# A four-layer graph stack on one Trainium2 core: variances of the layernorms in four segments, node rows and dense adjacency blocks written during mixing, and a first part of the convolution ahead of its product

## The chip, the cores and the metric

The kernel runs on one core of one Trainium2 chip. The metric is the device time of one execution in microseconds (us); lower is better. Five engines work side by side, each through its own list of instructions in order: PE multiplies matrices, DVE and ACT do vector work and can read PE's results, POOL does vector work and issues gathers, and SP issues plain memory transfers. A thing that one engine makes and another reads is handed over by a semaphore.

## The reference

Eight graphs of 2048 nodes with 64 features each share one adjacency matrix. Four layers each add their result to x, after a layernorm without weights and a relu:

```python
def _layernorm(x, axis=-1, eps=1e-5):
    m = jnp.mean(x, axis=axis, keepdims=True)
    v = jnp.var(x, axis=axis, keepdims=True)
    return (x - m) / jnp.sqrt(v + eps)
...
    h = jnp.maximum(_layernorm(x, axis=-1), 0.0)
    x = x + _L0_gnn_ref(h, ...)
    h = jnp.maximum(_layernorm(x, axis=-1), 0.0)
    x = x + _L1_gnn_ref(h, adj, L1_gnn_embedding, L1_gnn_weight, L1_gnn_bias)
    h = jnp.maximum(_layernorm(x, axis=-1), 0.0)
    x = x + _L2_gnn_ref(h, adj, ...)
    h = jnp.maximum(_layernorm(x, axis=-1), 0.0)
    x = x + _L3_gnn_ref(h, adj, L3_gnn_weight, L3_gnn_a, L3_gnn_bias)
```

Layer 0 is a hypergraph attention g and an industry average (a product with the adjacency), mixed by a softmax over two tanh scores. Layer 1 is the one that most of the change concerns:

```python
        As = [jnp.eye(N, dtype=x.dtype)]
        if K > 1:
            As.append(A)
        for _ in range(2, K):
            As.append(2.0 * (A @ As[-1]) - As[-2])
        A_stack = jnp.stack(As, 0)
        x_g = jnp.einsum('knm,bmc->bnkc', A_stack, x)
        out = jnp.einsum('bnki,nkio->bno', x_g, w)
        return out + b
```

Here K is 3 and the weights w of a node are a mixture of 16 sets by the node's embedding. Layer 2 makes three rounds of messages over the adjacency, layer 3 is an attention over neighbours.

## The kernel before

**Layout.** Features stand on the partitions, two graphs at a time: a tile is 128 partitions (2 graphs x 64 features) by nodes, and q (0 to 3, `NP`) counts the four pairs. Nodes go in 4 chunks of 512 (`CW`) or 16 tiles of 128 (`P`). "Node rows" are the transposed form, one node on a partition with 512 columns. Six large buffers, `q0` to `q5`, and some more by stage are shared by name (`Slots`).

**The norm.** `norm_parts` (L275) is a generator, so that callers can put other work between its halves. First half, for each pair: PE subtracts the mean (a product with `center`), ACT squares, relu on DVE or ACT. Then four products with `to_rows` (L261) put the variances of pair q into two rows of a group of 32 partitions, 512 columns; ACT takes the root (L290), DVE the reciprocal (L291). Second half, for each pair: a product with `from_rows` (L266) spreads the two rows over 128 partitions, and the caller's `write` multiplies. There are 17 norms: 4 at the start, beside the check of the adjacency (`check_adj`), 4 in mixing, 4 in the convolution and 5 in the third layer (`Scores.chunk`, the last two with 256 columns).

**Mixing** (`mix`, L695). For each chunk and pair, PE makes the scores p1 (two tiles of two PSUM banks), ACT their tanh, PE the difference pd (one bank), ACT t2, DVE the mixture. Three more banks, `bank`, serve everything else: the transposes that `each` makes of gathered rows, and the norm of the chunk before, whose halves are stepped at pairs 0 and 1. Work given as `beside` is stepped once a pair: `Lists.fill` (L2507), which gathers 60 blocks of the adjacency by index, four at a time, and stores them as `cells` in bfloat16. The write of the norm (L706) puts its result into `xe` and `xo`. x of the last chunk goes to buffers `q4`, `q5`.

**Second layer** (`layer1_near`, L1642). It begins with `lists.load`: three dense blocks of rows of the adjacency and 13 blocks called `zero` are loaded and cast to bfloat16. Then `xe` and `xo` are transposed to node rows `ah` (in `q4`, `q5`), which are also stored to `sent[0]`. The first adjacency product follows tile by tile (`Feed`): for each target a dense part with the three hub tiles, and a listed part, for which POOL gathers rows of `sent[0]`, ACT and DVE split each into two parts (L2630, L2631), and PE multiplies. `turn` transposes the result back. `acc` has three PSUM banks there.

**Convolution** (`convolution_near`, L1697). It loads its weights, then makes the second product for the first chunk whole (`product(0)`), then for each chunk and pair 16 outputs `pk` (8 blocks of weights, 2 halves, six banks): a product with w01 opens the bank, one with w2 on the second product closes it, DVE adds the bias and multiplies by the embedding (L1852), and POOL sums (L1858, the last block on DVE). Pieces of the next chunk's product are stepped in between.

**Order.** The program's order is the one written, but the scheduler may put an instruction earlier in its engine's list when its inputs are ready; `behind` keeps the order of those given to it. A buffer that is used again makes its next writer wait for the last reader.

Of the kernel before, what the change touches and what calls it, by code (L numbers as in the profile page):

```python
# [19 lines left out]
P = 128  # L20
NB = 8
# [4 lines left out]
R = P // NP  # L26
CW = 512
# [19 lines left out]
F16 = mybir.dt.float16  # L47

# [86 lines left out]
class Kernel:  # L135
# [76 lines left out]
    def setup(self):  # L212
# [19 lines left out]
        self.to_rows = c.tile([P, R], F, name="to_rows")  # L232
        nc.vector.memset(self.to_rows, 0.0)
        self.from_rows = c.tile([P, 2, D], F, name="from_rows")
        for s in range(2):
            nc.vector.memset(self.to_rows[s * D : (s + 1) * D, s : s + 1], 1.0 / D)
        for q in range(NP):
            r = slice(R * q, R * (q + 1))
            nc.vector.tensor_copy(
                self.from_rows[r],  # L240
                self.ident[r, R * q : R * q + 2].unsqueeze(2).to_broadcast([R, 2, D]),
            )
# [18 lines left out]
    def to_pair_rows(self, out, stationary, src):  # L261

        for q in range(NP):
            self.mm(out[R * q : R * (q + 1)], stationary, src(q))

    def from_pair_rows(self, out, q, rows):  # L266

        r = slice(R * q, R * (q + 1))
        self.mm(out, self.from_rows[r].rearrange("r s f -> r (s f)"), rows[r])
# [5 lines left out]
    def norm_parts(self, ch, x, xr, sq, std, bank, write, relus=None):  # L275
# [12 lines left out]
        pv = bank()  # L288
        self.to_pair_rows(pv, self.to_rows, lambda q: sq[:, q])
# [3 lines left out]
        for q in range(NP):  # L293
            pr = bank()
            self.from_pair_rows(pr, q, std)
# [377 lines left out]
    def x_ind(self, slots, k):  # L673
        w_ind = self.block_diag(k, self.a["W_ind"], "w_ind")
        x_ind = Split(slots, "x_ind", ("q7", "q6", "q9", "q8"))
        hn = self.h[0]
        with self.tc.tile_pool(reuse_waits="tile", name="x_ps", bufs=3, space=PSUM) as ps:
# [17 lines left out]
    def mix(self, slots, ind, g, fcw, av, each=None, beside=None):  # L695
# [17 lines left out]
        with (  # L713
# [6 lines left out]
            def attend(ch, q):  # L720
# [9 lines left out]
                if q == 0:  # L730
                    bufs[ch] = end if ch == NC - 1 else [b[:, ch % 2] for b in big]
# [15 lines left out]
            for ch in range(NC):  # L747
                s = slice(ch * CW, (ch + 1) * CW)
                x, sq, xr = bufs[ch]
                for q in range(NP):  # L750
# [22 lines left out]
                    if q < 2:  # L773
                        next(norm, None)
                    next(beside, None)
                self.store_x(0, ch, x)
                std = w.tile([P, CW], F, name="std")
                norm = self.norm_parts(ch, x, xr, sq, std, bank, write, nc.scalar)
            for _ in norm:
                pass  # L780
            for _ in beside:
# [9 lines left out]
    def layer0_pairs(self, slots, far):  # L791
# [8 lines left out]
        with tc.tile_pool(reuse_waits="tile", name="k0", bufs=1) as k:  # L800
# [3 lines left out]
            with (  # L804
# [46 lines left out]
                x_ind = self.x_ind(slots, k1)  # L851
# [42 lines left out]
            )  # L894
            with tc.tile_pool(reuse_waits="tile", name="filling", bufs=1) as w:
                self.mix(slots, ind, h_t, fcw, av, each, lambda bank: self.lists.fill(cells, w))
# [119 lines left out]
    def layer0(self, slots):  # L1016
# [14 lines left out]
        with tc.tile_pool(reuse_waits="tile", name="k0", bufs=1) as k:  # L1031
            x_ind = self.x_ind(slots, k)
# [609 lines left out]
    def layer1_near(self, slots, k2, far):  # L1642
# [11 lines left out]
        with (  # L1654
            tc.tile_pool(reuse_waits="tile", name="cheb", bufs=2) as w,
# [1517 lines left out]
```

## Time and profile before

| what | value |
|---|---|
| median of 3 runs | 2005.93 us (2004.48 to 2013.83) |
| profiled execution | 2004.73 us, of which the span of the profile is 2003.0 |
| mean granted PE clock | 0.91 |
| busy, share of the span | PE 85%, DVE 70%, POOL 52%, ACT 40% |
| start and check of the adjacency | 0 to 101 us |
| hypergraph attention, lists, industry product | 101 to 458 |
| mixing | 458 to 593.5 |
| transposes to node rows, dense blocks | 593.5 to 611.3 |
| first product of the second layer | 611.3 to 721 |
| second product for the first chunk | 721 to 767 |
| convolution with the rest of the second product | 767 to 1245 |
| third layer | 1245 to 1710 |
| fourth layer | 1710 to 2003 |

Times in the table by stage are from the span's start, read from the first and last instruction of a line. A busy PE is not PE at its peak, since matmuls are pipelined; and idle time of an engine that isn't the bound costs nothing.

### The profile page before, as it was taken

What the parts mean: (1) busy time and instruction counts of PE and PEld (TensorE: products, weight loads), DVE (VectorE), ACT (ScalarE), POOL (GpSimd) and SP (SyncE); (2) the same over time, 40 slices, a digit from 0 to 9 for tenths busy, and PEclk for the clock granted to TensorE, in tenths of its full rate; (3) what the DMA queues carried; (4) which work ended last, traced back from release to release, by engine and by line L of the source; (5) the groups of instructions that cost most, each with busy time, mean ns of one, the idle gap of its engine ahead of it and who ended that gap; (6) DMA issues with size and microseconds to landing.
All of it is one profiled execution on the core that took longest, in us unless ns stands there. A gap on an engine that the chain in (4) does not pass through costs nothing. (4 is left out here: it accounts for less than half of the span.)

```text
span 2003.0 us, 22362 instructions
## 1 busy us (share of the span) xinstructions
PE 1712.0 (85%) x7094; PEld 986.7 (49%) x7098; DVE 1393.1 (70%) x2281; ACT 811.0 (40%) x1634; POOL 1036.1 (52%) x1005
## 2 busy tenths in 40 slices
PE   6888999898977779999999998678789899378985
PEld 2446766663325544444434443567576575244432
DVE  6888788864776657676776556698787566257874
ACT  5722545445555643221110101555556553176400
POOL 1101466668734645875765453553664440657870
PEclk8888999999887979999999899889899898689997
DMA  9641223336247864232320211667687674845665
GB/s 340 260 117 44 74 95 111 106 111 202 58 135 225 242 190 123 74 116 63 85 80 32 79 48 63 214 198 253 199 261 244 184 241 136 261 117 172 172 177 193
DMA packets 125882, 305.21 MB, mean 152 GB/s; under 512 B 29345, under 2 KB 33201, under 8 KB 120241
## 3 DMA queue, kind: packets, MB, share of 16 engines
q0 software_dynamic: 45328, 149.60, 25.0%
q1 hardware_dynamic: 78112, 149.80, 22.4%
q10 hardware_dynamic: 2304, 4.20, 0.6%
q8 instruction: 60, 0.98, 0.2%
q14 instruction: 78, 0.63, 0.1%
HBM read 240.40 MB, written 63.14 MB: 152 GB/s over the span
## 5 line engine op out<-in xcount | busy, mean ns | idle before, releaser
L2613 POOL DMA_INDIRECT raw<-sent,index x300 | 315.0, 1050 | 343.0 <-DVE part_lo L2631 137.7
L2631 DVE TENSOR_TENSOR part_lo<-raw,part_hi 128x512 fp32r<-128x512 f32 x352 | 266.2, 777 | 142.9 <-ACT part_hi L2630 77.4
L2630 ACT CAST part_hi<-raw 128x512 fp32r<-128x512 f32 x352 | 212.2, 619 | 333.1 <-PE acc L176 223.5
L1858 POOL TENSOR_TENSOR half<-half,y 128x512 f32<-128x512 f32 x192 | 247.6, 1319 | 135.0 <-DVE y L1852 134.3
L176 PE MATMUL pk<-q,w 128*128 128x512 f32 (+1 forms) x768 | 301.9, 610 | 2.3 <-DVE q L1742 0.9
L176 PE MATMUL acc<-q,ident 128*128 128x512 f32 x416 | 205.9, 620 | 25.3 <-issue 12.1
L176 PE MATMUL acc<-part_hi,weights 128*128 128x512 f32 x365 | 179.3, 495 | 31.8 <-ACT part_hi L2630 17.6
L176 PE MATMUL acc<-part_lo,weights 128*128 128x512 f32 x365 | 168.6, 464 | 36.2 <-DVE part_lo L2631 27.2
L1852 DVE SCALAR_TENSOR_TENSOR y<-pk,bias,q 128x512 f32<-128x512 f32 x224 | 157.8, 743 | 55.1 <-PE pk L176 36.1
L176 PEld LDWEIGHTS pk<-q,w 128*128 128x128 f32 (+1 forms) x768 | 115.9, 190 | 156.1 <-issue 121.0
L2862 POOL DMA_INDIRECT ring<-f_rows,near x121 | 138.9, 1148 | 71.0 <-issue 30.5
L176 PEld LDWEIGHTS acc<-q,ident 128*128 128x128 f32 x416 | 77.4, 196 | 102.0 <-issue 63.2
L176 PEld LDWEIGHTS acc<-part_lo,weights 128*128 128x128 f32 x365 | 75.1, 206 | 86.9 <-DVE part_lo L2631 50.5
L176 PEld LDWEIGHTS acc<-part_hi,weights 128*128 128x128 f32 x365 | 75.0, 206 | 82.4 <-issue 48.0
L2340 POOL TENSOR_TENSOR q<-q,beta 128x512 f32<-128x512 f32 x57 | 76.1, 1337 | 71.3 <-DVE beta L2316 32.9
L176 PE MATMUL pp<-adj,x_ind_hi 128*128 128x512 f32 x256 | 90.5, 470 | 0.5 <-DVE q L864 0.3
L2933 DVE TENSOR_TENSOR q<-ring,e 128x1024 f32<-128x1024 f32 x58 | 69.9, 1218 | 20.7 <-remote 10.0
L2599 ACT CAST hub_weights<-dense 128x384 fp32r<-128x384 bf16 x80 | 40.6, 511 | 104.1 <-PE acc L176 96.9
L2340 POOL TENSOR_TENSOR q<-q,coef 128x512 f32<-128x512 f32 x57 | 63.1, 1108 | 21.2 <-DVE q L2363 16.9
L291 DVE RECIPROCAL std<-std 128x512 f32<-128x512 f32 (+1 forms) x17 | 53.7, 3161 | 27.3 <-ACT std L290 23.4
L176 PE MATMUL pp<-adj,x_ind_lo 128*128 128x512 f32 x256 | 72.0, 400 | 0.0
L2524 POOL DMA_INDIRECT listed_raw<-in_adjT_dram,cell x60 | 62.2, 1037 | 16.5 <-issue 15.8
(501 smaller groups left out, 3430.8 us busy)
## 6 DMA issues: line engine op xcount, KB each, us to landing
rows<-in_adj_dram SPq DMA_DIRECT2D x16, 1024.0 KB
adj_t<-in_adjT_dram SPq DMA_DIRECT2D x64, 256.0 KB
own<-sent SPq DMA_DIRECT2D x52, 256.0 KB
raw<-sent SPq DMA_DIRECT2D x52, 256.0 KB
sent<-u SPq DMA_DIRECT2D x48, 256.0 KB
q<-x SPq DMA_DIRECT2D x9, 1024.0 KB
links<-squares POOLq DMA_DIRECT2D x16, 512.0 KB
x<-q SPq DMA_DIRECT2D x8, 1024.0 KB
```

The lines of the kernel that those rows point to most:

```text
L176: self.nc.tensor.matmul(out, lhsT, rhs, start=start, stop=stop)
L291: nc.vector.reciprocal(std, std)
L1852: nc.vector.scalar_tensor_tensor(y, pks[b, half], bias[:, b : b + 1], emb[:, b], op0=OP.add, op1=OP.mult,)
L1858: add.tensor_add(acc, acc, y)
L2340: self.nc.gpsimd.tensor_tensor(x, x, by.unsqueeze(2).to_broadcast([P, NB, D]), op=OP.mult)
L2524: self.kern.behind(nc.gpsimd.indirect_dma_start(raw[:, i], None, rows, bass.IndirectOffsetOnAxis(ap=self.cell[:, c + i : c + i + 1], axis= ...
L2599: self.nc.scalar.copy(to, self.lists.dense[:, :, i * P : (i + 1) * P])
L2613: self.nc.gpsimd.indirect_dma_start(raw, None, self.rows[:], bass.IndirectOffsetOnAxis(ap=self.lists.index[:, c : c + 1], axis=0),)
L2630: nc.scalar.copy(hi, raw)
L2631: nc.vector.tensor_sub(lo, raw, hi.bitcast(F))
L2862: self.nc.gpsimd.indirect_dma_start(to, None, self.kern.f_rows[:], bass.IndirectOffsetOnAxis(ap=index, axis=0))
L2933: nc.vector.tensor_tensor(y.rearrange("n i (b f) -> n i b f", b=NB), block[:, i : i + 2, : NB * D].rearrange("n i (b f) -> n i b f", b=NB) ...
```

## The change

- The variances of a norm go into four segments. A segment is a quarter of the columns. `to_rows` is wider (32+6 columns), and segment i is multiplied with a shifted part of it, so that its rows land two partitions further on; four products accumulate into one bank of 128 columns. Root and reciprocal run on 128 columns. The spreading takes a segment's two rows with `from_rows[:, i]` and writes a quarter of the bank.
- `mix` takes `turned`: at pairs 2 and 3 of a chunk the four node tiles of the chunk before are transposed from `xe`, `xo` into `ah` and stored to `sent[0]`, two a pair; the last four after the last norm. x of the last chunk uses the ring of buffers like the others.
- `fill` also loads the dense and zero blocks, in 16 pieces of 512 columns, and ACT copies them; cells, dense and zero are held as bytes. `load` is gone.
- The new class `Conv` holds weights and the embedding's buffer and is made ahead of the first product; embeddings are loaded at the ninth tile. For pair 0 of the first chunk `first_part` makes the products with w01 alone, adds the bias, multiplies and sums on DVE: 8 of 16 pieces after the first product, the rest between the pieces of `product(0)`. Later the products with w2 open their own banks, and are multiplied and added.
- PSUM: the two products and the convolution share one pool; `acc` and `side` have two banks together.
- The industry weights have their own pool (`x_ind`); the third layer's attention reuses the tile `mine` for its first output.

```diff
-        self.to_rows = c.tile([P, R], F, name="to_rows")
+        self.to_rows = c.tile([P, R + 2 * SEG - 2], F, name="to_rows")
         nc.vector.memset(self.to_rows, 0.0)
-        self.from_rows = c.tile([P, 2, D], F, name="from_rows")
+        self.from_rows = c.tile([P, SEG, 2, D], F, name="from_rows")
         for s in range(2):
-            nc.vector.memset(self.to_rows[s * D : (s + 1) * D, s : s + 1], 1.0 / D)
+            at = 2 * SEG - 2 + s
...
+            nc.vector.memset(self.to_rows[s * D : (s + 1) * D, at : at + 1], 1.0 / D)
         for q in range(NP):
             r = slice(R * q, R * (q + 1))
             nc.vector.tensor_copy(
-                self.from_rows[r],
-                self.ident[r, R * q : R * q + 2].unsqueeze(2).to_broadcast([R, 2, D]),
+                self.from_rows[r].rearrange("r i s f -> r (i s) f"),
+                self.ident[r, R * q : R * q + 2 * SEG].unsqueeze(2).to_broadcast([R, 2 * SEG, D]),
...
-        pv = bank()
-        self.to_pair_rows(pv, self.to_rows, lambda q: sq[:, q])
+        n = sq[:, 0].shape[-1] // SEG
+        std = std[:, :n]
+        parts = [slice(i * n, (i + 1) * n) for i in range(SEG)]
+        pv = bank()[:, :n]
+        for i, c in enumerate(parts):
+            at = 2 * (SEG - 1 - i)
+            self.to_pair_rows(
+                pv, self.to_rows[:, at : at + R], lambda q: sq[:, q][:, c], start=i == 0,
+                stop=i == SEG - 1,
+            )
         nc.scalar.activation(std, pv, AF.Sqrt, bias=self.eps)
         nc.vector.reciprocal(std, std)
         yield
         for q in range(NP):
             pr = bank()
-            self.from_pair_rows(pr, q, std)
+            for i, c in enumerate(parts):
+                self.from_pair_rows(pr[:, c], q, std, i)
             write(q, ch, xr[:, q], pr)
...
+                    last = ch == NC - 1 and turned is None
+                    bufs[ch] = end if last else [b[:, ch % 2] for b in big]
...
+                    elif ch > 0 and turned is not None:
+                        for i in range(2):
+                            turned((ch - 1) * TC + 2 * (q - 2) + i, bank)
...
+            if turned is not None:
+                for t in range(NT - TC, NT):
+                    turned(t, bank)
...
+            def turned(t, bank):
+                s = slice(t * P, (t + 1) * P)
+                for i, (src, h) in enumerate(((xo, slice(D, P)), (xe, slice(0, D)))):
+                    pt = bank()[:, : NP * D].rearrange("n (q f) -> n q f", q=NP)
+                    for q in range(NP):
+                        nc.tensor.transpose(pt[:, q], src(q)[h, s], self.ident[h, h])
+                    self.copy(columns(ah(t), i), pt)
+                nc.sync.dma_start(self.sent[0][s], ah(t))
...
-            lists.load(w)
-            hub = Hub(w, "first_hub")
-            for t in range(NT):
-                s = slice(t * P, (t + 1) * P)
-                for i, (src, h) in enumerate(((xo, hi), (xe, lo))):
-                    pt = ps.tile([P, NP, D], F, name="pt", tag=("acc", "pz")[i], bufs=3)
+            conv = Conv(self, slots, k, ps)
+            with tc.tile_pool(reuse_waits="tile", name="cheb", bufs=2) as w:
+                hub = Hub(w, "first_hub")
+                for t in range(HUBS):
+                    hub.fill(self, t, ah(t))
+
+                def turn(t):
+                    s = slice(t * P, (t + 1) * P)
+                    pz = ps.tile([P, NP, P], F, name="pz", tag="pk", bufs=6)
                     for q in range(NP):
-                        nc.tensor.transpose(pt[:, q], src(q)[h, s], ident[h, h])
-                    self.copy(columns(ah(t), i), pt)
-                nc.sync.dma_start(self.sent[0][s], ah(t))
-                if t < HUBS:
-                    hub.fill(self, t, ah(t))
...
+                    if t == NT // 2:
+                        conv.begin()
+                turn(NT - 1)
+                for _ in range(8):
+                    next(conv.early)
...
             for _ in product(0):
+                next(conv.early, None)
+            for _ in conv.early:
                 pass
...
+                                if not begun:
+                                    self.mm(pk, w01[half][:, c], src(q)[:, s], stop=False)
...
-                                self.mm(pks[b, half], w2[h, c], aah[h, q], start=False)
+                                self.mm(pks[b, half], w2[h, c], aah[h, q], start=begun)
...
+                                new = begun or b > 0
+                                y = w.tile([P, CW], F, name="y", bufs=3) if new else acc
+                                if begun:
+                                    nc.vector.tensor_mul(y, pks[b, half], emb[:, b])
+                                else:
+                                    nc.vector.scalar_tensor_tensor(
+                                        y, pks[b, half], bias[:, b : b + 1], emb[:, b],
+                                        op0=OP.add, op1=OP.mult,
+                                    )
+                                if new:
+                                    own = b == NBLK - 1
+                                    add = nc.vector if own else nc.gpsimd
                                     add.tensor_add(acc, acc, y)
                         if q == NP - 1 and not ends:
...
+        def take():
+            if blocks:
+                to, src = blocks.pop(0)
+                raw = w.tile([P, CW], F, name="block_raw", bufs=3)
+                if len(src.shape) == 3:
+                    raw = raw.rearrange("p (i n) -> p i n", n=P)[:, : src.shape[1]]
+                nc.sync.dma_start(raw, src)
+                taken.append((to, raw))
+
+        def store():
+            to, raw = taken.pop(0)
+            self.kern.behind(nc.scalar.copy(to, raw))
...
+            if len(taken) > 1:
+                store()
+            take()
...
+    def first_part(self):
+
+        nc = self.nc
+        s = slice(self.CHUNKS[0] * CW, (self.CHUNKS[0] + 1) * CW)
+        for q in range(self.EARLY):
+            for b in range(NBLK):
+                for half, src in enumerate(self.xs):
+                    pk = self.bank()
+                    self.kern.mm(pk, self.w01[half][:, b * P : (b + 1) * P], src(q)[:, s])
+                    acc = self.accs[q][half]
+                    y = self.k.tile([P, CW], F, name="early_y", bufs=2) if b else acc
+                    nc.vector.scalar_tensor_tensor(
+                        y, pk, self.bias[:, b : b + 1], self.emb[:, b], op0=OP.add, op1=OP.mult,
+                    )
+                    if b:
+                        nc.vector.tensor_add(acc, acc, y)
+                    yield
...
-        o = w.tile([P, NB * D], F, name="first_o")
+        o = mine[:, : NB * D]
```

## The prediction

> **What bounds the kernel now.** The program has stages with different limits, so I read the busy time of each engine by stage first, then the order of time at the places where an engine stands still, then the groups for durations. The busy shares by stretch (columns: stretch, its length, then busy us and count of PE, PE weight loads, DVE, ACT, POOL, then the granted PE clock, DMA share, GB/s):
>
> ```profile
> 458.00:490.00 32.00, 30.93 (x117) 11.99 (x118) 15.29 (x23) 20.37 (x28) 26.72 (x25) 0.92 0.53 178
> 490.00:522.00 32.00, 27.73 (x102) 8.83 (x97) 22.92 (x29) 17.82 (x25) 26.58 (x25) 0.95 0.37 112
> 522.00:555.00 33.00, 30.89 (x106) 10.10 (x105) 22.87 (x31) 19.76 (x28) 23.16 (x21) 0.90 0.24 69
> 555.00:593.50 38.50, 27.50 (x83) 6.90 (x81) 26.08 (x31) 18.06 (x26) 13.98 (x17) 0.86 0.33 101
> 593.50:616.00 22.50, 15.98 (x139) 14.44 (x140) 15.00 (x27) 12.37 (x30) 0.00 (x0) 0.50 0.78 274
> 721.00:767.00 46.00, 33.16 (x100) 18.75 (x100) 18.67 (x29) 17.30 (x35) 16.91 (x16) 0.80 0.67 194
> 767.00:860.00 93.00, 90.75 (x296) 41.93 (x292) 72.59 (x87) 24.46 (x50) 71.53 (x57) 1.00 0.28 79
> ```
>
> The first four rows are mixing: PE is busy 117 of 135.5 us, and 11 of its 18.5 idle us lie in the last row. In 593.5 to 616 (the transposes to node rows at the head of the second layer) POOL does nothing and the PE clock is 0.50. 721 to 767 is the product ahead of the convolution: PE has 13 us free. From 767 on, PE is full. The order of time shows the end of mixing and the head of the second layer (start, us, engine, line, what, and in brackets the idle time before it and who ended it):
>
> ```profile
> 582.49 3.35 DVE L291 RECIPROCAL std<-std 128x512 f32<-128x512 f32 x1 [3.20 <-ACT std L290]
> 585.89 1.91 PE L176 MATMUL bank<-std,from_rows 32*128 32x512 f32 x6 [4.83 <-DVE std L291]
> 587.81 5.67 DVE L710 TENSOR_TENSOR q<-q,bank 64x512 f32<-64x512 f32 x8 [1.97 <-PE bank L176]
> 610.71 0.93 ACT L2599 CAST hub_weights<-dense 128x384 fp32r<-128x384 bf16 x2 [5.79 <-DVE dense L2547]
> 611.27 0.79 PE L176 MATMUL acc<-first_hub_h,hub_weights 128*128 128x512 f32 x1 [4.22 <-ACT hub_weights L2599]
> ...
> 617.96 1.34 POOL L2613 DMA_INDIRECT raw<-sent,index  x1 [45.76 <-DMA sent<-q]
> ```
>
> Here the last norm's reciprocal is waited for by PE; the first product starts 17.8 us after the last norm write (593.5), held by the cast of the dense block, and the first gather waits for the last node row to land. The view of one tile, the norms' deviation, gives the reciprocal (duration in ns: least, median, most; first and last start; forms). The chain of waits (start, us, what) shows where it is exposed late, and what eight matmul instructions of 128 columns take:
>
> ```profile
> L291 DVE RECIPROCAL std<-std x17: 1742/3353/3353, 21.0 to 1689.8; 128x512 f32<-128x512 f32 x15, 128x256 f32<-128x256 f32 x2
> ```
>
> ```profile
> 1444.68 0.89 PE pn L176 x8
> ...
> 1682.22 1.66 DVE std L291
> 1689.85 1.67 DVE std L291
> ```
>
> **What the Trainium skill says.** "ScalarE: Activation LUTs", section "What ACT_TABLE_LOAD costs": one element per cycle for fp32 and bf16 alike, 0.833 ns per element. The square root of this trace agrees: 687 ns at 512 columns, 474 at 256, 0.832 ns each. "TensorEngine Tiling", section "Key Properties": tiles of the array load weights and multiply in parallel. The trace agrees: the 8 matmul instructions of one spreading (4 pairs, two instructions each, 32 rows each) take 1.14 us at 1240.36, where 8 of full height on the same bank size (the centering) take 3.70. The same page, "Instruction Overhead", says that a matmul has a floor of about 60 cycles, so cutting columns by four doesn't cut cost by four. "TensorE: Matmul & The Clock Gate", section "What's actually happening": the clock is halved after an idle window of about 3.4 us. The trace agrees: 0.50 after the idle PE of 579 to 593.
>
> **The change part by part.** All sums are against the profiled execution: span 2003.0, time 2004.73.
>
> *Variances in four segments.* The reciprocal is linear: (3353-1742)/256 = 6.29 ns a column, so 128 columns take 1742-128x6.29 = 0.94 us: 2.41 less at each of 15, 1.21 less at the two of 256 columns. The root loses 0.32 us (384x0.832 ns). Against this PE gets 32 small instructions for 8, twice: the sums (128x32) and the spreading (32x128). No row shows these shapes. Nearest from below: streaming is unchanged, so nothing; from above: 32 one after the other at the 0.111 us of a 128-column instruction (8 in 0.89 us at 1444.68), 3.55 us instead of 1.1, +2.4 on each. I take +0.3 for the sums, since four pairs alternate there and can run side by side, and +1.0 for the spreading, since four segments of a pair follow each other on the same rows.
> - Start (four norms beside the adjacency check). DVE is busy 9.3, 9.7, 7.7, 7.0, 10.0, 7.8 of each 10 us from 20 to 80 and 11.9 of the last 12. The first two savings go into waits for adjacency rows (5.7 us at 44). The third and fourth shift the last comparison and the features behind the last spreading: 2.4+1.5, less 0.9 for PE. I take -3 (0 to -8).
> - Mixing, three inner norms: the reciprocal ends at 530.66, and the next DVE step on the path (t2 ready at 531.59) comes later; likewise at 498.4 and 563.4. Hidden, so 0.
> - Convolution, three inner norms: PE is the bound, +1.3 each, less the 0.8 us PE stalled at 930 behind the reciprocal: +2 together (0 to +10). The last norm (1236.23 to 1240.36) is exposed: -2.7+0.7 = -2.
> - Third layer: inner norms +2 on PE (-2 to +7); the two exposed ones -1.2-0.2+0.9 each, -1 together (-3 to +1).
>
> *Weights of the industry product in a pool of their own.* Their load was issued at 117, the first use is at 190.9. Now it can't precede the release of memory used by the list preparation, just ahead. Memset 0.2, two issues 1.2, landing: +1.5 (0 to +4).
>
> *Node rows and dense blocks move into mixing.* Removed at 593.5 to 611.3: 128 transposes, 32 copies (ACT 0.375, DVE 0.42), three casts of 1.23 and one of 1.02 on DVE, four loads, 16 stores. Put into the loop: 96 transposes (0.073 us each, 56 in 4.1: 7 us PE), 24 copies (4.5 us ACT, 5 us DVE), 16 ACT copies of 512 columns into bytes (0.6 each, 9.6 us; byte operands aren't in the trace, the length is that of other casts, range 0.3 to 1.0), 16 block loads and 12 stores on SP. On SP these pass x's loads and stores; a store waits for its two copies, and behind it queues the next x load. That is hidden: the load for the third chunk was issued at 490.2 and needed at about 519; for the fourth, which now shares the second's buffer, it can issue at 523 and is needed at about 547. PE before 555 has only 7.5 us idle, in short waits at other places, so the 7 us count almost in full: +8 for the loop (+2 to +30). Four tiles remain after the last norm: 32 transposes 2.4 us, copies beside them, so about 3.5 us to the last row and 1 to the first product: 17.8-4.5 = 13.3 saved; reciprocal and root of the last norm another 2.7, less 0.7 for spreading at a low clock: 15.3 by the first product. By the first gather it is more: the last row's store lands 4.5 us after its issue (613.5 to 618), so 8 us after the last norm write instead of 24.5: 18.5 with the same 2. I take -17, between the two (-10 to -20). What is late next is the gather chain itself, 60 gathers at 1.25 us on POOL.
>
> *Second layer's body.* Accumulators go from three banks to two, so less work is begun ahead: +1 (0 to +5). Convolution weights (6 loads, 1.5 MB, 3.1 us of DVE) come earlier on SP, beside the head, with no reader there. Embedding loads start at the ninth tile instead of 639: the first reader is after 711, hidden.
>
> *First part of the convolution ahead.* Sixteen products with the first weights (2 instructions of 0.43, 13.8 us) leave the first quarter of the first chunk. Six of them were already issued early (735.61, 12 instructions). So PE can gain 8.6 us. But DVE gets 16x0.743+14x0.69 = 21.5 us in a stretch where it has 18.7 of 46, less 3.1 moved away: 37 of 46, so splits of gathered rows queue behind it. In the first quarter DVE then needs 18 us plus seven or so splits and POOL 14 adds of 1.27 = 17.8 us, where that quarter lasted 27 us (767.3 to 794.1): 20 is the floor. I take -4 (+8 to -9).
>
> *Third layer's tail* reuses a dead tile: 0; nothing else is hidden under it.
>
> Sum: -3+0+2-2+2-1+1.5+8-17+1-4 = -12.5. So 2004.7-12.5 = 1992.2 by the profiled execution; the median of the runs shown is 1.2 above it, so 1993.
>
> **The rivals.**
> 1. *Mixing swallows it* (slower). Three banks serve transposes, centering, sums and spreading, and half of the copies that free a bank stand in ACT's queue behind pairs of tanh (2.12 us) and byte copies. If each of the 12 ACT-freed banks of the loop stalls PE by 2.1 us or more and the clock drops, the loop costs 8+25 = +33: sum +12.5, 2018. It decides from 31 us on (faster by nothing at 20.5). For it: PE waited 2.2 us for such banks at 501.9. Against: ACT is busy only 18 to 20 of 32 us.
> 2. *The early part is given back* (no change): the products for the first chunk run DVE-bound, +2 instead of -4, and spreading costs PE 0.8 us more in each of the six inner norms of the convolution and third layer: +6+5, sum -1.5, 2004. For it: 37 of 46 us on DVE. Against: PE was half-clocked and blocked there already.
> 3. *More gain*: the transposes of mixing fill PE's waits (loop +2), and the first quarter reaches its floor with DVE hidden (-9): -23.5, 1982.
>
> **How the numbers follow.** Forecast (1986 to 1997) 0.42, rival 3 0.20, rival 2 0.20, rival 1 0.18. A measurement of this kernel can tell about 0.5%, 10 us, from no change: faster is rival 3 and nine tenths of the forecast, 0.58; same the rest of it and rival 2, 0.24; slower 0.18. Range: 1977 to 2010; it leaves out most of rival 1 and the far end of rival 3. The forecast's own range is 1986 to 1997.
>
> **What would show it.** The reciprocal near 0.94 us x15; sums and spreading of one norm within 1.0 to 1.5 and 1.6 to 2.6 us on PE; mixing's last norm write at 593-3+1.5+8-2 = 597.5 and the first product within 5 us of it, the first gather within 9; the first quarter of the convolution about 20 us. It is wrong if mixing runs more than 20 us longer, if PE shows idle time over 3 us inside it, or if the convolution starts later after the second layer's last product than the 46 us of now by more than 6.

## The result, and the profile after

Measured beside each other, 22 runs each: the kernel before 2004.6 us in the median (1993.78 to 2015.62), the changed kernel 2008.1 (1995.83 to 2021.18), ratio 1.0031 (95% interval 1.0011 to 1.0051). The change is slower by 0.3%. I had forecast 1993, faster by 0.6%; the time lies in my range, the direction was wrong. That it lies in the range is in part luck: the third layer became 12.3 us shorter where I had 2, for a reason that stays open; with my 2 the time would have been near 2018. The profiled span went from 2003.0 to 2007.4.

I read the order of time at the places of my terms first. The busy time by stretch, over the stages that the prediction showed of the kernel before (columns as there; mixing in the first four rows, its end and the head of the second layer in the fifth):

```profile
477.00:512.00 35.00, 33.88 (x149) 11.97 (x145) 17.21 (x24) 23.89 (x34) 29.23 (x28) 0.92 0.52 173
512.00:549.00 37.00, 32.47 (x153) 14.55 (x152) 23.31 (x33) 19.53 (x32) 26.42 (x26) 0.86 0.45 142
549.00:587.00 38.00, 34.15 (x185) 15.46 (x183) 20.40 (x33) 22.25 (x36) 19.01 (x18) 0.87 0.45 136
587.00:605.00 18.00, 17.26 (x122) 8.32 (x122) 11.57 (x18) 11.74 (x18) 12.32 (x12) 1.00 0.30 82
605.00:624.40 19.40, 15.06 (x118) 10.99 (x114) 13.28 (x24) 11.22 (x25) 0.49 (x3) 0.77 0.38 139
```

A chunk of mixing now takes 35 to 38 us where it took 32 to 33, and PE is busy for 32 to 34 of them. The stretch between mixing and the second layer is shorter, though POOL still does next to nothing in it (0.49 of 19.40 us): the order of time on PE shows the last norm and the first product close together.

```profile
614.21 4.78 PE L178 MATMUL bank<-std,from_rows 32*128 32x128 f32 x32 [2.10 <-DVE std L302]
...
621.16 2.73 PE L925 MATMUL bank<-ident,q 64*128 64x64 f32 x25 [0.36 <-DVE q L725]
624.41 0.79 PE L178 MATMUL acc<-first_hub_h,hub_weights 128*128 128x512 f32 x1 [0.52 <-ACT hub_weights L2615]
```

The wait for the reciprocal fell from 4.83 to 2.10 us, and the view of the deviation's tile has the length that I predicted (0.94):

```profile
L302 DVE RECIPROCAL std<-std x17: 552/952/953, 23.1 to 1688.2; 128x128 f32<-128x128 f32 x15, 128x64 f32<-128x64 f32 x2
```

So the parts that the change names work. The loss begins at the other end, in the start: its last step, the first scores product, moved from 101.5 to 111.7. The third norm there, on DVE, before (first lines) and after (second):

```profile
54.13 0.69 DVE L285 TENSOR_SCALAR xr<-bank 128x512 f32<-128x512 f32 x1 [0.77 <-ACT sq L282]
56.45 3.35 DVE L291 RECIPROCAL std<-std 128x512 f32<-128x512 f32 x1 [1.62 <-ACT std L290]
59.72 2.23 DVE L381 SCALAR_TENSOR_TENSOR equal<-rows,squares 128x2048 bf16<-128x2048 f32 x1
...
61.87 2.48 DVE L630 TENSOR_TENSOR q<-xr,bank 128x512 f32<-128x512 f32 x4
```

```profile
57.89 1.40 DVE L288 TENSOR_SCALAR xr<-bank 128x512 f32<-128x512 f32 x2
61.46 2.29 DVE L393 SCALAR_TENSOR_TENSOR equal<-rows,squares 128x2048 bf16<-128x2048 f32 x1 [2.17 <-ACT squares L392]
...
63.68 0.95 DVE L302 RECIPROCAL std<-std 128x128 f32<-128x128 f32 x1
...
66.85 0.69 DVE L642 TENSOR_TENSOR q<-xr,bank 128x512 f32<-128x512 f32 x1
67.87 0.69 DVE L642 TENSOR_TENSOR q<-xr,bank 128x512 f32<-128x512 f32 x1 [0.33 <-PE bank L178]
68.89 0.69 DVE L642 TENSOR_TENSOR q<-xr,bank 128x512 f32<-128x512 f32 x1 [0.33 <-PE bank L178]
```

Two things are new. The scheduler has put a comparison of an adjacency row (`equal`) ahead of the reciprocal; that comparison waits 2.17 us for ACT's squares and takes 2.29, so the shorter reciprocal starts later after its norm than the long one did. Before, the comparison stood behind the reciprocal and found its squares ready, and PE spread beside it. And each write now waits for PE: the writes start 1.02 us apart and take 0.69. At the clock of this place, half of full speed in both traces, PE takes 5.10 us for a norm's spreading where it took 2.09 (first line before, second after):

```profile
80.32 2.09 PE L176 MATMUL bank<-std,from_rows 32*128 32x512 f32 x8 [2.15 <-DVE std L291]
```

```profile
88.71 5.10 PE L178 MATMUL bank<-std,from_rows 32*128 32x128 f32 x32
```

The second loss is the industry weights. POOL's list has their memset (the filling of their tile with zeros) behind four gathers of the list preparation (205.55), SP issues the loads at 205.81, and PE stands still for them:

```profile
208.78 16.47 PE L178 MATMUL pn<-w_ind,q 128*128 128x128 f32 x128 [6.56 <-DMA w_ind<-in_W_ind_dram]
```

### The profile page after: what moved, and what is told of

The parts are those of the page before. It is cut to its first block, busy times and chain, and to the rows that moved or that the text cites. A ratio compares the mean times of both kernels' runs of the same rounds, so it can differ in the third digit from the quotient of the medians.

```text
span 2007.4 us, 24062 instructions
## 1 busy us (share of the span) xinstructions
PE 1735.0 (86%) x7910; PEld 1043.1 (52%) x7914; DVE 1375.6 (69%) x2307; ACT 814.7 (41%) x1650; POOL 1044.5 (52%) x1007
## 3 DMA queue, kind: packets, MB, share of 16 engines
q8 instruction: 66, 1.08, 0.2%
## 5 line engine op out<-in xcount | busy, mean ns | idle before, releaser
L178 PE MATMUL pk<-q,w 128*128 128x512 f32 (+1 forms) x768 | 307.0, 619 | 0.3 <-DVE q L288 0.2
L1856 POOL TENSOR_TENSOR half<-half,y 128x512 f32<-128x512 f32 x180 | 230.9, 1312 | 117.4 <-DVE y L1849 116.7
L1849 DVE SCALAR_TENSOR_TENSOR y<-pk,bias,q 128x512 f32<-128x512 f32 x210 | 148.0, 743 | 58.3 <-PE pk L178 40.9
L2958 POOL DMA_INDIRECT ring<-f_rows,near x121 | 140.4, 1161 | 73.6 <-issue 29.9
L2615 ACT CAST hub_weights<-dense 128x384 fp32r<-128x384 uint8 x80 | 40.4, 511 | 86.6 <-PE acc L178 81.7
L2355 ACT ACTIVATE q<-q 128x512 f32<-128x512 f32 x57 | 36.0, 631 | 78.2 <-DVE q L2353 78.1
```

What stands on the lines that cost most here:

```text
L178: self.nc.tensor.matmul(out, lhsT, rhs, start=start, stop=stop)
L1849: nc.vector.scalar_tensor_tensor(y, pks[b, half], bias[:, b : b + 1], emb[:, b], op0=OP.add, op1=OP.mult,)
L1856: add.tensor_add(acc, acc, y)
L2355: nc.scalar.activation(e, d, AF.Relu, scale=-1.0)
L2615: self.nc.scalar.copy(to, self.lists.dense[:, :, i * P : (i + 1) * P])
L2958: self.nc.gpsimd.indirect_dma_start(to, None, self.kern.f_rows[:], bass.IndirectOffsetOnAxis(ap=index, axis=0))
```

## The experiments

Twelve runs were made in four groups, on different occasions and chips; beside them the kernel before had medians of 1994.9, 2001.7, 1953.9 and 1993.9 us. So totals are compared as ratios to it, and lengths of stages come from the profiles. Ratios of different groups carry more scatter than their intervals say: the changed kernel alone had 1.0031 and 1.0084. Both kernels were profiled twice (E5, E6): the start and the tail repeat within 1.5 us, lists within some 3, mixing within some 4. Kernels with the same code in a stage show more: the start took 103.7, 101.1 and 99.5 us in E1, E7 and E8, and mixing 123.3 us in E11 against 131.8 and 128.4 in the changed kernel. In the third group (E9 to E11) the third layer's later rounds and the fourth layer were shorter in all three kernels, so the column of the third layer is not compared across groups.

Lengths in us, from the first or last start of the instructions named: start (to the first scores product), lists (from there to the first low part of the adjacency product), mixing (first tanh to last centering), tail (to the second layer's first product), conv (second product's start to the convolution's last bias), third (to the first product of the third layer's second round).

| kernel | start | lists | mixing | tail | conv | third | ratio (95%) |
|---|---|---|---|---|---|---|---|
| before | 101.5 | 114.9 | 117.8 | 32.6 | 510.2 | 162.8 | |
| E6 before again | 100.2 | 114.6 | 121.9 | 31.1 | 512.4 | 161.0 | 1.0002 (0.9979-1.0025) |
| changed | 111.7 | 120.9 | 131.8 | 15.0 | 509.8 | 148.9 | 1.0031 (1.0011-1.0051) |
| E5 changed again | 112.5 | 117.8 | 128.4 | 15.0 | 512.7 | 150.3 | 1.0084 (1.0051-1.0117) |
| E1 one segment, early weights | 103.7 | 112.3 | 128.5 | 18.5 | 513.8 | 152.8 | 0.9978 (0.9958-0.9998) |
| E2 one segment | 101.3 | 118.4 | 129.7 | 18.6 | 512.1 | 148.3 | 1.0017 (0.9987-1.0047) |
| E3 segments alone | 112.3 | 125.6 | 118.9 | 29.9 | 508.0 | 155.0 | 1.0061 (1.0038-1.0084) |
| E4 spreading by twos | 108.3 | 124.6 | 130.3 | 15.0 | 513.1 | 153.7 | 1.0016 (0.9993-1.0038) |
| E7 no early part | 101.1 | 114.7 | 130.5 | 18.6 | 502.8 | 155.1 | 0.9931 (0.9908-0.9954) |
| E8 turned after mixing | 99.5 | 114.8 | 124.1 | 27.7 | 515.5 | 157.3 | 0.9992 (0.9968-1.0016) |
| E9 two segments | 108.2 | 116.4 | 124.7 | 16.3 | 501.1 | 149.5 | 0.9925 (0.9902-0.9949) |
| E10 bytes alone | 99.9 | 114.9 | 115.4 | 33.1 | 510.1 | 152.7 | 1.0001 (0.9985-1.0017) |
| E11 changed, no early part | 114.6 | 122.3 | 123.3 | 15.0 | 495.7 | 148.0 | 0.9963 (0.9945-0.9982) |
| E12 segments where exposed | 102.6 | 115.1 | 130.3 | 16.8 | 501.1 | 152.4 | 0.9887 (0.9839-0.9935) |

**E1 and E2: is it the segments, or where the weights lie?** Both are the changed kernel with `SEG = 1`; E1 also loads the industry weights from the early pool again.

```diff
-SEG = 4
+SEG = 1
...
-                x_ind = self.x_ind(slots)
+                x_ind = self.x_ind(slots, k1)
...
```

> The changed kernel with one segment per norm (32 instructions fall back to 8 in each sum and spreading) and the industry weights loaded from the early pool as in the kernel before; mixing, the second layer's head and the early part of the convolution stay changed. Theory A (the segments cost PE more than the reciprocal saves: spreading 2.82 us instead of 1.13 at full clock, 5.1 instead of 2.1 at half): the first scores product comes back from 111.7 to 101.5 +-2, the first product with the industry weights from 208.8 to about 191, mixing's inner chunks from 40 and 38 to about 37, and the total is 1990 +-5, below both kernels. Rival R1 (mixing's added transposes and byte copies are the loss, the norms are neutral): the start comes back by less than 3, mixing stays at 40 and 38, total 2003 to 2008. Rival R2 (the placement of the weights is the loss): start unchanged, weights back by 6, total about 2001.

> The changed kernel with one segment per norm, everything else changed, the industry weights in their late pool. Against the run with early weights it isolates that pool. Theory A with the late load costing what the trace suggests (load 3 us behind the release, 6.6 us of idle PE): +5 to +6 at the first product with these weights, of which the adjacency product that follows keeps 3 to 5; total 1993 to 1996. My sum on record had +1.5. If it is hidden, the two runs agree within 2.

The start came back (103.7 and 101.3), with the weights too in E1 (first use at 190.5). E1 is faster than the kernel before, barely. Mixing did not come back, as R1 had it: its loss is not the segments'. E2 against E1: the late pool costs 6.1 us at the adjacency product (118.4 to 112.3), not my 1.5; E7 and E8, which have E1's start and lists, took 114.7 and 114.8, so 4 to 6. From the first scores product to the first product with these weights it is 94.6 us in E2 and 86.8 in E1.

**E3: the segments alone.** The kernel before with the new `norm_parts`, and with what the larger `from_rows` (1.5 KB more a partition) forces for space: weights late, `mine` reused, cells as bytes.

> The kernel before with the four segments alone, and what their larger constants force for space: the industry weights in the late pool, the reused tile in the third layer, gathered blocks held as bytes. Theory A: first scores product at 111 to 113, first product with the industry weights at 208 to 210, mixing 4 to 8 us longer by PE (spreading +1.1 for three pairs, more where the clock falls), the convolution's norms within 2 of before, total 2012 to 2022, slower than both kernels. Rival R1: start within 3 of before, total 2002 to 2008. Both have the last norm of mixing and of the convolution faster by 2 to 3.

Start 112.3, lists 10.7 longer: Theory A's signs, and slower by 0.6%. But mixing is 118.9, unchanged (I had expected 4 to 8 more): the inner norms of mixing are hidden, as the prediction had it. The ratio of 1.006 fits the 2012 to 2022 that I expected, beside 2004.6 for the kernel before.

**E4: the price of spreading.** The changed kernel, with two pairs' products alternating:

```diff
-        for q in range(NP):
-            pr = bank()
+        for two in range(0, NP, 2):
+            prs = [bank(), bank()]
             for i, c in enumerate(parts):
-                self.from_pair_rows(pr[:, c], q, std, i)
-            write(q, ch, xr[:, q], pr)
+                for j, pr in enumerate(prs):
+                    self.from_pair_rows(pr[:, c], two + j, std, i)
+            for j, pr in enumerate(prs):
+                write(two + j, ch, xr[:, two + j], pr)
```

> The changed kernel, but the spreading of two pairs alternates: segment by segment, first one pair's product and then the other's, into two banks, so that neighbouring instructions use different rows of the array. Theory A1 (instructions on the same 32 rows follow each other, a weight load of 0.187 us can't go beside the product before it): 32 instructions take 1.4 to 1.8 us at full clock instead of 2.82, start 4 to 7 us earlier, total 1998 to 2003. Rival A2 (an instruction costs 0.088 us wherever it is, 2.82/32): still 2.7 to 2.9, total within 3 of the changed kernel, or later since the writes of a pair start later.

One norm of the convolution at full clock, in the kernel before, the changed one and E4:

```profile
1044.47 1.23 PE L176 MATMUL pk<-std,from_rows 32*128 32x512 f32 x8
```

```profile
945.60 2.82 PE L178 MATMUL pk<-std,from_rows 32*128 32x128 f32 x32
```

```profile
945.02 1.72 PE L178 MATMUL pk<-std,from_rows 32*128 32x128 f32 x32
```

A1 holds at this place: 0.088 us an instruction when a pair's eight follow each other on the same 32 rows, 0.054 when two pairs alternate. "TensorE: Matmul & The Clock Gate" of the Trainium skill, section "The mechanism", says that a weight load overlaps with products under way only where the row groups differ. The trace agrees: in E4 the instructions of two pairs start together, 0.006 us apart, while those of one pair stay 0.11 us apart, as in the changed kernel. My price had not used this. The page's section "Back-to-back issue gap" gives about 81 ns a product in a stream of loads and products at 128 columns; the measured 0.11 us on one row group is longer, and the 0.088 is a mean that counts places where two pairs overlap, so its nearness to 81 shows nothing. Each pair also writes its own bank, and no run tells the bank from the rows.

In the start the spreading fell from 5.10 to 3.10 us, yet only 3.4 us of the 10 came back.

**E5 and E6: how far do stages repeat?**

> The changed kernel once more, beside the other runs of this call. Nothing is changed; it shows how far a stage's length differs between two profiles of one kernel. The start (first scores product) should be within 1 us of 111.7, mixing within 2 of 128.7 from the first tanh to the last centering. If the third layer's first part (end of the convolution to the first product of its second round, 148.9 us in the changed kernel, 162.8 in the kernel before) is the scheduler's other order, it stays within 3 of 148.9; if it is luck of the gathers, it moves by 5 or more.

> The kernel before once more, for its stages: start 101.5 +-1, mixing 118.4 +-2 from the first tanh to the last centering. Third layer's first part: 162.8 +-3 if the kernel before has the worse order of instructions there, anything from 148 to 163 if that length is luck of the gathers.

The start and the third layer's length repeat in both (111.7 and 112.5, 101.5 and 100.2; 148.9 and 150.3, 162.8 and 161.0), mixing moves by 3 to 4 (by the measure of the table the first profile of the changed kernel has 131.8, not the 128.7 of my expectation). So the 11 to 14 us that the third layer gained are not an accident of one profile.

**E7 and E11: the early part of the convolution.** E1, and the changed kernel, each without it (the loop that steps it may then find nothing left):

```diff
-                    next(conv.early)
+                    next(conv.early, None)
...
-    EARLY = 1
+    EARLY = 0
```

> One segment, early weights (the first run of the call before), and the early part of the convolution taken out: the first quarter makes its own products with the first weights again, as in the kernel before. Theory A (rival 2 of the record: the early part is given back, since DVE carries 21 us more in the product and the first quarter is held by POOL's 14 sums and DVE beside them): from the second product's start to the second quarter 73 to 76 us instead of 77.5, total 1 to 4 below that run. Rival (the early part saves PE 8 us as I summed): 81 to 86, total 4 to 8 above it.

> The changed kernel with four segments and late weights, without the early part of the convolution alone. Theory A (the early part costs 8 to 10 us wherever it is, by DVE in the product and POOL's sums in the first quarter): from the second product's start to the last block of the convolution 500 to 504 instead of 510 to 513, total 8 to 10 below the changed kernel, so about level with the kernel before. Rival (its cost hung on the one-segment norms around it): 508 to 513, total within 4 of the changed kernel.

The time from the second product's start to the last bias falls from 513.8 to 502.8 in E7, and from 509.8 and 512.7 to 495.7 in E11, and both kernels become faster than the one before (0.9931, 0.9963). So the early part costs 11 us or more, more than even Theory A had. The whole column agrees: every kernel with the early part took 509.8 to 515.5, E7, E9, E11 and E12 without it 495.7 to 502.8. Stretches of E1, which has it, and of E7 (three of the product and the first half of the first quarter, which is the first chunk's first pair; columns as above):

```profile
715.70:730.00 14.30, 14.03 (x41) 7.04 (x41) 13.45 (x24) 4.32 (x10) 4.70 (x5) 1.00 0.54 183
730.00:745.00 15.00, 12.97 (x39) 6.95 (x37) 14.92 (x24) 6.38 (x13) 10.21 (x7) 0.89 0.39 122
745.00:764.80 19.80, 13.92 (x52) 9.65 (x54) 8.54 (x15) 9.35 (x19) 4.73 (x5) 0.83 0.65 200
764.80:779.00 14.20, 11.21 (x31) 4.03 (x27) 13.45 (x16) 3.61 (x7) 13.45 (x10) 0.80 0.25 77
```

```profile
714.80:730.00 15.20, 12.85 (x44) 7.66 (x43) 6.44 (x14) 6.45 (x14) 7.33 (x8) 0.89 0.60 208
730.00:745.00 15.00, 12.74 (x49) 7.37 (x47) 8.59 (x14) 9.97 (x21) 9.09 (x9) 1.00 0.75 220
745.00:755.70 10.70, 8.46 (x20) 4.62 (x22) 3.30 (x5) 3.40 (x7) 0.00 (x0) 0.54 0.55 184
755.70:769.00 13.30, 13.30 (x47) 6.02 (x44) 12.64 (x14) 3.65 (x8) 8.81 (x6) 0.99 0.25 79
```

With it DVE is full in the second stretch (14.92 of 15), and the product takes 49.1 us instead of 40.9. PE is busy for 6.9 us more in it and idle for 8.2 instead of 6.9: the added products filled none of its waits. That DVE is the reason is read from its full row and from POOL's gathers, which waited 9.6 us for splits in this product and 3.3 in E7's; no run gives the early part's vector work to another engine. In the first quarter POOL is full (13.45 of 14.20) and PE, which has less to do there, gains nothing: 28.4 us against 26.9.

But why is E7 also shorter than the kernel before? There the product took 48.3. Its weights were loaded from 715.4 on and DVE was done with them at 738.7, in the middle of the product, and six products with them stood in PE's list as one block; ACT's next cast waited behind the product after them (PE, then ACT, of the kernel before):

```profile
735.61 7.49 PE L176 MATMUL pk<-q,w 128*128 128x512 f32 x12 [0.38 <-PE acc L176]
742.54 0.79 PE L176 MATMUL acc<-hub_h,hub_weights 128*128 128x512 f32 x1
```

```profile
744.54 0.52 ACT L2599 CAST hub_weights<-dense 128x384 fp32r<-128x384 bf16 x1 [8.34 <-PE acc L176]
```

In E7 the weights are long there, and the same 12 instructions stand in PE's waits for gathered rows, from 720.21 on as six, then in twos.

```profile
720.21 2.82 PE L178 MATMUL pk<-q,w 128*128 128x512 f32 x6
...
726.25 1.91 PE L178 MATMUL pk<-q,w 128*128 128x512 f32 x2
```

This is read from the order of time. No run moves the weights alone; the bytes alone left the product at 48.3 us (E10), while E9, E11 and E12, with early weights and no early part, had 38.6 to 39.9.

**E8: what of mixing is the node rows?** E1 with all 16 tiles turned after the last norm.

> One segment, early weights, and all 16 node tiles transposed and stored after the last norm, none inside mixing; the dense blocks stay in mixing. From the first tanh to the last centering it was 129.0 with the tiles inside and 118.4 before. Theory A (the 96 transposes and 24 copies in the loop cost PE their length and the bank waits): 120 to 122, of 10.6 some 7 to 9 are theirs and 2 are the block copies; the tail then takes 13 to 14 us for 128 transposes where 32 took 3.5, total 2 to 6 above the first run of the call before. Rival B (the byte copies on ACT and their loads stretch the loop): 126 to 129, total 8 or more above.

Between the two: mixing 124.1, so 4.4 of E1's excess of some 9 us would be the tiles', and the rest is left for the block copies and their loads, which no run takes out. The tail takes 9.2 more. The total is 0.14% above E1's ratio, inside the intervals. Mixing and tail together are 147.0 in E1 and 151.8 here, but 149.1 in E7, whose mixing is E1's: the tiles inside mixing are worth 3 to 5 us, no more than mixing scatters by.

**E9 and E12: do segments pay anywhere?** E9 is E7 with two segments and spreading by twos; E12 uses these in the four norms alone whose reciprocal PE waits for.

```diff
-            for two in range(0, NP, 2):
+        step = 2 if seg > 1 else 1
+        for two in range(0, NP, step):
...
+                    ch, x, xr, sq, std, bank, write, nc.scalar, SEG if ch == NC - 1 else 1
```

> The kernel without the early part (one segment, early weights, ratio 0.9931), with two segments of 256 columns for each norm, and the spreading of two pairs alternating; the smaller constants leave room for the early weights. Theory A (what counts is PE's time, 16 instructions where 8 were, against 1.6 us less reciprocal where it is exposed): spreading 1.0 to 1.5 us at full clock, start within 2 of 101, mixing's tail 1 to 2 shorter, total within 4 of that kernel, so not measurably better. Rival (fewer columns for the reciprocal do pay once PE's price is cut): 4 to 10 below it.

> The kernel of the run with two segments (no early part, early weights, spreading by twos), but the segments are used in four norms alone: the last of mixing, the last of the convolution and the two last of the third layer, where the trace shows PE waiting for the reciprocal. The other 13 norms have one segment. Theory A (segments pay only where the reciprocal is waited for, and cost elsewhere): start back from 108.2 to 101 +-2, first use of the industry weights from 199.1 to 190 or 191, mixing's tail kept at 16 to 17, ratio to the kernel before 0.987 to 0.992. Rival (the 7 us at the start are made good later, since the stages up to mixing wait for the same adjacency rows): ratio 0.992 to 0.994, as with two segments everywhere.

E9 is the most telling miss: PE spreads a norm in 2.11 us in the start, as in the kernel before, and still the start takes 108.2, not 101. The same norm on DVE in E9:

```profile
58.41 1.39 DVE L288 TENSOR_SCALAR xr<-bank 128x512 f32<-128x512 f32 x2
62.52 2.29 DVE L395 SCALAR_TENSOR_TENSOR equal<-rows,squares 128x2048 bf16<-128x2048 f32 x1 [2.71 <-ACT squares L394]
...
64.74 1.75 DVE L302 RECIPROCAL std<-std 128x256 f32<-128x256 f32 x1
...
68.71 2.48 DVE L644 TENSOR_TENSOR q<-xr,bank 128x512 f32<-128x512 f32 x4
```

The writes no longer wait for PE, but the comparison still stands ahead of the reciprocal. E12, with one segment there, has the old order and 102.6. The traces agree on this throughout: with segments in the start, the reciprocal of each of the four norms begins 0.5 to 2.4 us after the root, behind a comparison; without, it begins at once in three of them and 1.0 us after the root in the fourth. By subtraction the order accounts for some 6 of the 10 us (E9 less E12) and the spreading for 3 to 4 (E4). These are estimates, of the size by which equal starts scatter, and no run keeps the old order with segments in.

E12 has the lowest ratio, 1.1% under the kernel before: it has the node rows in mixing, early convolution weights and no early part. Its interval overlaps those of E7 and E9, so the totals don't tell whether its segments pay. The tail does: 18.5 and 18.6 us with one segment (E1, E7), 16.8 and 16.3 with two (E12, E9), 15.0 with four.

**E10: the bytes.** The kernel before with `cells` held as bytes and nothing else.

> The kernel before, with the gathered blocks held as bytes and nothing else changed, looked at for the third layer's first part (162.8 and 161.0 us in the two profiles of the kernel before; 155.0 in the one with segments alone, which has these bytes and the same order of gathers there; 148 to 153 in those where the scheduler puts the first gather of links after 9 instead of 16 others). Theory C (the bytes make those 7 us, by the casts that read them): 154 to 157. Rival D (an order of instructions, or the later arrival of that stage): 160 to 164.

No change in total (1.0001). For the third layer it decides nothing: 152.7 lies below both ranges, nearer to Theory C's, but this group was fast in the rounds after it in all three kernels, and it has no profile of the kernel before.

## Why the prediction was wrong

My sum was -12.5; the spans differ by +4.4, and with the second pair of profiles by +4.6. Term by term, means of the two pairs:

| term | predicted | measured |
|---|---|---|
| start | -3 (0 to -8) | +11.2 |
| weights of the industry product | +1.5 | +4.6; 6.1 from E2 less E1 |
| adjacency product | 0 | -0.6 |
| mixing loop | +8 | +10.3 |
| tail of mixing, head of second layer | -17 | -16.9 |
| second layer's body | +1 | -1.2 |
| early part, with the convolution's inner norms | -4, +2 | 0 |
| convolution's last norm, third layer to its second round | -2 | -12.3 |
| rest of the third layer, its norms | +1 | +5.5 |
| fourth layer | 0 | +3.9 |

**The step that failed is the start's**, "2.4+1.5, less 0.9 for PE. I take -3": it is 14 us off, and with -3 the sum would have kept its sign. That the segments make the loss is shown: with one segment the start took 99.5 to 103.7 us, with the segments alone 112.3. I priced the spreading from a place at full clock (1.14 us for 8 at 1240.36), while the start's own row had 2.09 at 80.32 and became 5.10, and charged PE's share once, not in four norms with DVE waiting. And I took DVE's order as given, though the program lets the scheduler place instructions; that moved the reciprocal behind a comparison (some 6 us of the 10 by E9 less E12, an estimate).

**The early part** had two terms hidden in one -4. What it does itself is +11 (E1 to E7; 14 to 17 from the changed kernel to E11): I had seen DVE at 37 of 46 us, named it in rival 2, and let the PE figure decide. What made up for it is a gain I costed at nothing: the weights "come earlier on SP, beside the head, with no reader there". Their readers were the six products in PE's list, and E7's product, where that block is gone, is 7.4 us shorter (48.3 to 40.9); that the weights are the reason is argued from the order of time.

**The spreading** came out at 2.82 us at full clock (I said 1.6 to 2.6), the sums at 1.08 where all squares were ready, as said. So it is not the floor of about 60 cycles that made it dear: the sums, cut by four in the same way, kept their length. In the convolution the spreading stayed below what can be told (E3: 508.0). From the last reciprocal of the third layer to the fourth layer's first gather it took 23.3 us instead of 19.4: +4 where I had -1. Alternating pairs didn't help there (E4: 23.6); with two segments it was 18.2 (E12).

**Right**: the reciprocal (0.95), the tail in size and steps (first product 3.3 us after the last write ended, first gather 6.3, limits 5 and 9), the hidden norms of mixing, and the loop within its range. Of rival 1's waits, for banks that ACT frees, none came in the changed kernel's mixing. But the last write of mixing ended at 621.1, not at 597.5, and one of my signs of being wrong did show: PE idle for more than 3 us inside mixing, before the last pair of a norm's spreading, for a bank whose write DVE had begun late.

```profile
560.50 2.04 PE L178 MATMUL bank<-std,from_rows 32*128 32x128 f32 x8 [3.78 <-DVE q L725]
```

E5 has no such wait (2.2 us is the longest of its mixing) and a mixing 3.4 us shorter.

**Open**: the 12 us of the third layer. The exposed reciprocal has 2.7 of them (PE's wait 4.23 to 1.50), and a wait for the load of `aa`, 3.4 before, is absent after; but it is there in E7 with 2.5 us, and that stage is still shorter. The rest is spread over short waits for gathered rows, and no run isolates it. Every kernel with adjacency blocks as bytes took 148.0 to 157.3 us there, the two profiles without them 161.0 and 162.8. The order of POOL's gathers, which differs too, does not decide it: E3, E7 and E12 kept the order of the kernel before and took 152.4 to 155.1, E8 has the new one and took 157.3. The fourth layer's +3.9 is the mean of +2 and +6, and not explained.

## What to carry to other kernels

When a change swaps one long instruction for many short ones on another engine, price them at the clock and in the order of each place where they run, and look at what else the scheduler can put ahead of the shortened step: here both together gave back more than the reciprocal saved. Segments shortened the tail of mixing, where PE waited for the reciprocal, and lengthened the start. A load that comes earlier is worth what its late arrival blocked in the list of the engine that reads it; and before work is begun early, ask whether the engine that finishes it, here DVE, has room.

## What the runs showed of the hardware

- 32 instructions of 32 rows and 128 columns took 2.82 us at full clock with a pair's eight one after the other, 1.72 with two pairs alternating. Within a pair they started 0.11 us apart in both. At half clock it was 0.21 us in the changed kernel, with 128 columns in the start and with 64 at the third layer's end alike: there fewer columns made an instruction no shorter.
- The sums, with four groups of 32 columns of the array alternating, took 1.08 us for all 32 instructions of 128 columns (at 1138.82, all inputs ready), where 8 of 512 had taken 1.06 (at 1122.51). Splitting cost PE nothing there.
- In E1 the median split on DVE takes 0.69 us during the product and 1.34 in the first quarter, beside POOL's sums. In the whole trace the 321 splits that met no sum of POOL took at most 0.76 us, and the 30 over 1.0 us all met one. "SBUF — State Buffer" of the Trainium skill, section "SBUF: two separate sides", has a port pair that an operation of DVE with two inputs in SBUF and one of POOL that reads SBUF lock against each other; the trace agrees.
